# Layer 2's products of seven in a written order on all engines, with the fourth product later

## The chip, the cores and the metric

The kernel runs on one NeuronCore of a Trainium2 chip. TensorE (PE) multiplies matrices into PSUM banks, VectorE (DVE) and ScalarE (ACT) read those banks, GpSimd (POOL) works on SBUF only, and SyncE (SP) issues most DMAs. Each engine works through its own list of instructions in order and waits, where it must, for another engine. The metric is the device time of one execution in microseconds (us), as a median of runs.

## What is computed

Four layers work on x, 128 graphs of 64 nodes with 256 features; each is `x = layernorm(x + layer(x))`. Layer 0 is an attention over the adjacency, layer 1 an attention over 512 edges, layer 3 two graph convolutions and four LSTMs. The change lies in layer 2:

```python
agg = einsum('nm,bmd->bnd', A_hat, features)   # 8192 rows x 256
h   = relu(batchnorm(agg.reshape(-1, d) @ W1.T + b1, g1, be1))   # 256 -> 512
out = batchnorm(h @ W2.T + b2, g2, be2)                           # 512 -> 256
```

A batch norm takes mean and variance over all 8192 rows, so nothing behind it can start until every row has been multiplied and counted.

## The kernel before

**Blocks.** The 8192 rows stand transposed (features on partitions) as 16 blocks of 512 columns, `Aq(q)`, each with two halves of 128 features. The up multiplication makes `hidden(q, m)`, m = 0 to 3; the down multiplication makes `result(q, m)`, m = 0 and 1.

**Two ways to multiply.** A plain block (`up_block`, `up` and `put`, L721 to L742) takes 4 x 2 matmuls of 128 x 128 by 128 x 512; ACT adds the bias and DVE takes `bn_stats`. A job of seven (`class Seven`, L774, `seven`, L824) does a 2 x 2 by 2 x 2 product of tiles, for two blocks at once, with seven products instead of eight. It needs sums of the weight tiles (`weight_sums`, L747) and of the inputs (`tile_sums`, L833: three subtractions on POOL and one on DVE, in place). An up job (`up_job`, L846) has one term per product and covers one half g of the hidden features; a down job (`down_job`) has two terms, so two matmuls per product, and covers both results of two blocks.

**What the products need of each other.** Products 1 and 2 share one bank, products 6, 7 and 4 a second, products 5 and 3 a third. What ACT or DVE takes of a product has to be read before PE may add the next into that bank. Product 1 is copied by ACT (`kept`), product 6 is added to it by DVE (L801), product 5 is copied with its bias by ACT (L803), product 2 is finished by ACT (L805), product 3 by DVE (L808), product 7 by DVE (L812) and POOL (L813), product 4 by DVE (L816). The fourth product of a job is not done in that job: `seven` does it behind product 1 of the next job, from the list `late`. Each finished tile is counted by `bn_stats` on DVE (L849 up, L964 down).

**The order of the stages.** The program is written once, fully unrolled. Where nothing ties two instructions, a planner with its own estimates of durations fixes their order on each engine; `tc.issue_after` ties an instruction behind another on the same engine.

1. The last steps of layer 1 (`v_a`, `v_b`, `v_c`, the softmax of the last pair of blocks) are interleaved with entries of the list `fill`: plain blocks 0, 3, 4, 7, 8 and jobs for the pairs 1-2, 5-6 and 9-10. PSUM has five banks for them.
2. Plain block 11, then four up jobs: half 0 of pairs 12-13 and 14-15, then half 1 of both. From here there are eight banks. When the last job of a half has its fourth product, `finish` computes the scale and shift of batch norm 1 for that half (`normalisation`, L704).
3. `first(k)`, k = 0 to 3: the down multiplication of blocks 0 to 3, all eight banks open at once, one k after another. `relu` (L909, ACT) normalises and rectifies a tile in place. `prepare(4)` runs the relus and tile sums for the first down job beside it. At the end DVE takes the statistics and adds the bias (`leave`, L923).
4. Five down jobs for the pairs 4-5 to 12-13; during each one, `prepare` (or `ready`, for the last) is asked step by step for the relus and tile sums of the next pair. `done` stores both blocks to DRAM (`z_dram`, L968).
5. Plain down blocks 14 and 15, their statistics (L997), the bias additions (L923), `with_bias` (L930: the bias on the means) and `normalisation` of batch norm 2 for each half.
6. Layer 3 starts with the scale and shift of block 0 on ACT (L1144), transposes on PE (L1162), the addition to `x2r` (L1168), which SP loads from DRAM at that place (L1138), and a layer norm. All of layer 3 has its order written by hand by `given`, which ties every instruction behind the one called before it on its engine.

Of the kernel before, what the change touches and what calls it, by code (L numbers as in the profile page):

```python
# [41 lines left out]
def kernel(ctx: ExitStack, tc: tile.TileContext, i, out):  # L42
# [63 lines left out]
    bdT = const.tile([P, P], F32, name="bdT")  # L106

# [7 lines left out]
    with ExitStack() as two:  # L115
# [619 lines left out]
        def up_block(q):  # L735
            for m in range(2):
                put(q, m, up(q, m))
                if late:
                    late.pop(0).product(4)
            pz = [up(q, m) for m in (2, 3)]  # L740
            for m in (2, 3):
                put(q, m, pz[m - 2])  # L742
# [18 lines left out]
        kept_at = iter(range(10 ** 6))  # L761
# [12 lines left out]
        class Seven:  # L774

            def __init__(self, terms, bias, dst, stats, done=None, shape=lambda t: t):
                self.terms, self.bias, self.dst, self.stats, self.done = terms, bias, dst, stats, done
                self.shape = shape
                self.bank, self.kept = {}, {}

            def product(self, j):
                at = {1: 0, 2: 0, 6: 1, 7: 1, 4: 1, 5: 2, 3: 2}[j]
# [7 lines left out]
                self.use(j, self.bank[at])  # L790

            def keep(self, j):
                self.kept[j] = kept[next(kept_at) % len(kept)]
                return self.kept[j]

            def use(self, j, p_):
# [7 lines left out]
                elif j == 2:  # L804
                    nc.scalar.activation(dst(0, 0), shape(p_), AF.Identity, bias=self.bias(0))  # L805
                    self.stats(0, 0)
                elif j == 3:
                    nc.vector.scalar_tensor_tensor(dst(0, 1), shape(p_), self.bias(0), shape(k[6]),  # L808
                                                   op0=OP.add, op1=OP.add)
                    self.stats(0, 1)  # L810
                elif j == 7:
                    nc.vector.tensor_add(self.keep(7), p_, k[1])  # L812
                    nc.gpsimd.tensor_tensor(dst(1, 1), shape(k[7]), shape(k[5]), OP.add)  # L813
                    self.stats(1, 1)
                else:
                    nc.vector.scalar_tensor_tensor(dst(1, 0), shape(p_), self.bias(1), shape(k[1]),  # L816
                                                   op0=OP.add, op1=OP.add)
                    self.stats(1, 0)
                    if self.done:
                        self.done()  # L820
# [3 lines left out]
        def seven(job, feed=iter(())):  # L824
            job.product(1)
            if late:
                late.pop(0).product(4)
            for j in (6, 5, 2, 3, 7):
                job.product(j)
                next(feed, None)  # L830
            late.append(job)

# [9 lines left out]

        def inputs(q):
            return lambda k, n: Aq(q + n)[:, k * QT:(k + 1) * QT]

        def up_job(q, g, T, done=None):  # L846
# [4 lines left out]
                        lambda m: b1[:, 2 * g + m:2 * g + m + 1], dst, stats, done))  # L851
# [9 lines left out]
        fill = []  # L861
        for q in range(0, 8, 4):
            fill += [one(q), pair(q + 1, 0), one(q + 3), pair(q + 1, 1)]
        fill += [one(8), pair(9, 0), pair(9, 1)]
        sums_at = {0: 1, 4: 5, 8: 9}
        for n, (do, q) in enumerate([(v_b, NQ - LAG - 1), (v_c, NQ - LAG - 1)] + [
                (do, q) for q in range(NQ - LAG, NQ) for do in (v_a, v_b, v_c)]):
            if n in sums_at:
                T[sums_at[n]] = tile_sums(inputs(sums_at[n]))
            do(q, *[False] * (do == v_c))  # L870
            fill[n]()
# [8 lines left out]
        kept.append(wc.tile([P, QT], F32, name="kept4"))  # L880
# [12 lines left out]
        nc.sync.dma_start(bias2, i["L3_gnn_bhh"].rearrange("s (m p) -> p s m", p=P))  # L893

        assert q == NQ - LAST - 1
        up_block(q)
        ends = range(NQ - LAST, NQ, 2)
        T = {q: tile_sums(inputs(q)) for q in ends}
# [4 lines left out]
        for g in range(2):  # L903
            for q in ends:
                up_job(q, g, T[q], finish(g) if q == ends[-1] else None)
# [28 lines left out]
        def first(k):  # L934
            for q in range(LAST):
                relu(q, k)
                for m in range(M2):
                    if k == 0:
                        pz[q, m] = pbank()
                    down(q, m, pz[q, m], [k])  # L940
                    if late:
                        late.pop(0).product(4)
# [3 lines left out]
        def prepare(q):  # L946
            terms[q] = []
            for g in range(2):
                for k in range(2):
                    for n in range(2):  # L950
                        relu(q + n, 2 * g + k)
                    yield
                b = lambda k, n, g=g: hidden(q + n, 2 * g + k)
                a = lambda m, k, g=g: w2[:, 2 * g + k, m * P:(m + 1) * P]
                terms[q].append((a, [SW[1][:, n, g] for n in range(4)], b, tile_sums(b)))

        def ready(q):
            for k in range(M1):
                for n in range(2):
                    relu(q + n, k)  # L960
                yield

        def down_job(q, feed):
# [6 lines left out]
            seven(Seven(terms[q], lambda m: b2[:, m:m + 1], lambda m, n: result(q + n, m), stats, done, parts), feed)  # L970
# [4 lines left out]
        feed = prepare(LAST)  # L975
        for k in range(M1):
            first(k)
            next(feed, None)
        for _ in feed:
            pass  # L980
        for m in range(M2):
            for q in range(LAST):
                nc.vector.bn_stats(st2[:, m, q, :], pz[q, m])
                leave(q, m, pz[q, m])
            with_bias(m, 0, LAST)
        for q in range(LAST, NQ - 2, 2):
            down_job(q, prepare(q + 2) if q + 2 < NQ - 2 else ready(q + 2))
        ends = range(NQ - 2, NQ)
        pz = {}
        for m in range(M2):  # L990
            for q in ends:
                pz[q, m] = pbank()
                for k in range(M1):
                    down(q, m, pz[q, m], [k])
                    if late:
                        late.pop(0).product(4)
                nc.vector.bn_stats(st2[:, m, q, :], pz[q, m])  # L997
            if m == M2 - 1:
                for q in ends:
                    for n in range(M2):  # L1000
                        leave(q, n, pz[q, n])
            with_bias(m, NQ - 2, NQ)
            normalisation(sc2, sh2, st2, g2, be2, m)
# [18 lines left out]


    latest = {}

    def given(do, *args):
        traced = nc.cur_bb.bb.instructions
        first = len(traced)
        with ExitStack() as order:
            for e in latest.values():  # L1030
                order.enter_context(tc.issue_after(e))
            r = do(*args)
        for t in traced[first:]:
            if t.engine in (mybir.EngineType.PE, mybir.EngineType.DVE, mybir.EngineType.Activation,
# [615 lines left out]
```

## Time and profile before

| | us |
|---|---|
| three runs | 2067.59, 2071.39, 2072.15 |
| median | 2071.39 |
| profiled execution, its time | 2072.72 |
| profiled execution, its span | 2070.8 |
| mean granted clock | 0.982 |
| layer 2 in the trace, first to last matmul | 524.2 to 773.0 |

A row of the profile names a line of the kernel, an engine, an operation, and out<-in by the names of tiles. `pz` is a PSUM bank of layer 2, `Z` and `A` hold the hidden features, `SW` sums of weights, and `gath`, `lb`, `keep`, `wv`, `seg`, `w` and some of `Z` are rooms for the tile sums, taken over from layer 1. A float32 matmul stands as two records. A wait is put down to the instruction that ended it.

### The profile page before, as it was taken

Reading aid. Unit: us, or ns where it says so; the run is one execution under the profiler, and the core shown is the slowest. Engines: PE = TensorE matmul, PEld = TensorE weight load, DVE = VectorE, ACT = ScalarE, POOL = GpSimd, SP = SyncE. Lnnn points to the kernel's source line nnn. Section 1 sums busy time; section 2 is a strip of 40 time slices with the busy share of each in tenths; the row PEclk is TensorE's granted clock in tenths of the full one; section 3 lists DMA queues with packets and bytes.
Section 4 is the critical chain, followed back from the end, with each engine's and each line's share of the span. In section 5 each row is a group of like instructions: output and inputs, shape, how many; then the busy total and the mean of one; then the engine's idle time right before and its main releaser. Section 6 shows DMA issues by size and latency. Waiting matters only on the chain.

```text
span 2070.8 us, 31477 instructions
## 1 busy us (share of the span) xinstructions
PE 1961.5 (95%) x11579; PEld 1371.8 (66%) x11579; DVE 1209.8 (58%) x2702; ACT 959.9 (46%) x1840; POOL 808.4 (39%) x958
## 2 busy tenths in 40 slices
PE   5999999998899998999999999999999999999997
PEld 4666667675454335587678587687587687586675
DVE  7456666554567555574466674466674456443556
ACT  2766666665234713544343644343643343543333
POOL 1123343343534524273545253345253345123254
PEclk9999999999899998999999999999999999999998
DMA  5354343332202027351232532032522032301012
GB/s 148 66 69 70 72 76 53 55 54 44 34 21 39 24 93 245 130 191 52 87 132 68 183 113 92 11 131 69 182 86 79 1 119 71 128 1 76 1 62 72
DMA packets 235962, 170.69 MB, mean 82 GB/s; under 512 B 150560, under 2 KB 213536, under 8 KB 232480
## 3 DMA queue, kind: packets, MB, share of 16 engines
q1 hardware_dynamic: 233952, 166.72, 28.6%
q8 instruction: 91, 1.49, 0.3%
q0 software_dynamic: 1024, 1.05, 0.2%
q10 hardware_dynamic: 832, 0.92, 0.1%
q14 instruction: 63, 0.52, 0.1%
HBM read 107.82 MB, written 60.82 MB: 81 GB/s over the span
## 4 chain that ended last, share of the span: by engine, by line
PE 71%; DVE 14%; ACT 5%; POOL 4%; issue 3%; DMA 2%; SPq 1%; DVEq 0%; ACTq 0%; POOLq 0%
PE l L1392 26%; PE l L1357 9%; PE l L1249 8%; PE pz L788 4%; PE e L331 3%; PE m L303 2%; PE g L1212 2%; PE m L306 2%; PE z L340 2%; PE pz L727 2%; PE m L238 2%; PE m L421 2%; PE g L1127 1%; DVE cell L1336 1%; PE g L1200 1%
## 5 line engine op out<-in xcount | busy, mean ns | idle before, releaser
L1392 PE MATMUL l<-xs,wx 128*128 128x256 f32 (+1 forms) x896 | 276.8, 399 | 5.1 <-DVE gate L1411 3.9
L1392 PE MATMUL l<-hs,wh 128*128 128x256 f32 (+1 forms) x896 | 275.1, 399 | 3.1 <-DVE hs L1286 3.1
L86 POOL TENSOR_TENSOR ln_rs<-ln_rs,mhalf 128x2 f32<-128x2 f32 (+2 forms) x98 | 84.0, 857 | 436.8 <-DVE ln_rs L98 423.9
L1407 ACT ACTIVATE kept<-l 128x256 f32<-128x256 f32 (+1 forms) x224 | 88.6, 402 | 339.9 <-PE l L1392 338.6
L1392 PE MATMUL l<-H,wx 128*128 128x256 f32 (+1 forms) x672 | 210.2, 401 | 3.4 <-DVE gate L1420 3.4
L1392 PE MATMUL l<-hid,wh 128*128 128x256 f32 (+1 forms) x672 | 208.7, 399 | 0.0
L1392 PEld LDWEIGHTS l<-xs,wx 128*128 128x128 f32 x896 | 168.8, 190 | 49.5 <-POOL st L100 4.1
L1392 PEld LDWEIGHTS l<-hs,wh 128*128 128x128 f32 x896 | 169.3, 190 | 45.5 <-DVE hs L1286 5.7
L1357 PE MATMUL l<-H,wx 128*128 128x256 f32 (+1 forms) x768 | 187.9, 403 | 6.2 <-DVE H L1322 6.2
L1425 ACT ACTIVATE gate<-gate,bias 128x512 f32<-128x512 f32 (+1 forms) x280 | 170.5, 656 | 37.0 <-DVE gate L1416 31.0
L1357 PEld LDWEIGHTS l<-H,wx 128*128 128x128 f32 x768 | 146.8, 193 | 46.4 <-DVE H L1322 10.4
L1249 PE MATMUL l<-H,wih 128*128 128x512 f32 x384 | 167.9, 598 | 2.6 <-issue 2.6
L342 ACT ACTIVATE u<-z 128x1024 f32<-128x1024 f32 x128 | 130.4, 1025 | 63.2 <-PE z L340 62.1
L1392 PEld LDWEIGHTS l<-H,wx 128*128 128x128 f32 x672 | 126.0, 190 | 38.4 <-DVE gate L1420 7.3
L1392 PEld LDWEIGHTS l<-hid,wh 128*128 128x128 f32 x672 | 127.2, 190 | 32.0 <-issue 2.9
L1249 PEld LDWEIGHTS l<-H,wih 128*128 128x128 f32 x384 | 73.3, 192 | 93.2 <-issue 86.7
L1415 POOL TENSOR_TENSOR gate<-gate,kept 128x256 f32<-128x256 f32 (+1 forms) x84 | 65.2, 776 | 158.6 <-DVE kept L1413 158.6
L314 DVE TENSOR_TENSOR qs<-m,qs 64x256 fp32r<-64x256 f32 x128 | 54.0, 422 | 109.2 <-ACT qs L313 107.1
L1290 POOL TENSOR_TENSOR hs<-hid 128x256 f32<-128x256 f32 (+1 forms) x28 | 25.7, 916 | 200.0 <-DVE hid L1319 116.3
L340 PE MATMUL z<-gath_r,qs 128*128 128x512 f32 x256 | 100.5, 479 | 0.4 <-ACT u L342 0.2
L1344 ACT ACTIVATE gate<-cell 128x512 f32<-128x512 f32 (+1 forms) x88 | 58.6, 666 | 81.1 <-DVE cell L1336 58.8
L1409 DVE TENSOR_TENSOR gate<-l,kept 128x256 f32<-128x256 f32 (+1 forms) x112 | 49.1, 438 | 72.2 <-ACT gate L1425 44.1
(346 smaller groups left out, 3837.2 us busy)
## 6 DMA issues: line engine op xcount, KB each, us to landing
wx<-sums SPq DMA_DIRECT2D x9, 2048.0 KB
wh<-sums SPq DMA_DIRECT2D x9, 1792.0 KB
way<-st SPq DMA_DIRECT2D x54, 256.0 KB
st<-way SPq DMA_DIRECT2D x216, 64.0 KB
xin<-in_x SPq DMA_DIRECT2D x16, 512.0 KB
ld<-table SPq DMA_DIRECT2D x16, 512.0 KB
x_dram<-y SPq DMA_DIRECT2D x16, 512.0 KB
x2r<-x_dram SPq DMA_DIRECT2D x32, 256.0 KB
```

The lines of the kernel that those rows point to most:

```text
L86: nc.gpsimd.tensor_tensor(dst, dst, mhalf[:, :n], OP.pow)
L331: nc.tensor.matmul(pes[S][n * CG:(n + 1) * CG, :], apad[:, k, CG - HEADS - r0:2 * CG - HEADS - r0], u[:, k, :], start=r0 == 0 and k == 0, ...
L340: nc.tensor.matmul(z[:, k, :], L1[q]["qs"][c][:, s, k * P:(k + 1) * P], gath_r, start=True, stop=True)
L342: nc.scalar.activation(u, z, AF.Relu)
L788: nc.tensor.matmul(self.bank[at], lhs, rhs, start=first and n == 0, stop=n == len(self.terms) - 1, skip_group_check=True)
L1249: nc.tensor.matmul(b, wih1[:, k, mw * P:(mw + 1) * P], Hw[:, k], start=k == 0, stop=k == KD - 1)
L1344: nc.scalar.activation(tiles["g"][m], cell[:, m], AF.Tanh)
L1357: nc.tensor.matmul(one, w.raw[0][:, k, at, m, :], inp(r, 0, k)[:, g], start=k == 0, stop=k == KD - 1)
L1392: nc.tensor.matmul(self.banks[j], lhs, rhs, start=src == 0, stop=src == 1)
L1407: nc.scalar.activation(self.keep(j), b, AF.Copy)
L1415: e.tensor_tensor(t[0][:, 1], t[0][:, 1], k[5], OP.add)
L1425: given(lambda: nc.scalar.activation(dst, dst, f, bias=b))
```

## The change

- `given` moves to the top of the kernel, and with it layer 2 from block 11 on gets a written order on PE, DVE, ACT and POOL: each product, what is read of it, each relu, each sum and each statistic.
- Beside layer 1 there are seven plain blocks, 0 to 6, and the pairs 7-8 and 9-10.
- The fourth product and its two last statistics come later: in an up job behind product 5, in a down job behind product 6. `seven` takes them in steps (`tail`) from the job before.
- In an up job the third product is left to ACT and POOL instead of DVE. `kept` tiles have fixed places.
- The sums of the inputs of a down job come in two steps (`sums_in_order`), each in its place among the products. The relus of a pair are asked for in pairs, in six steps per job.
- In `first`, statistics and `leave` come block by block in the last k. In the last two blocks, block 14 leaves early, and block 15 is left by ACT behind the last normalisation in the program.
- `x2r` of blocks 0 and 1 is loaded while layer 2 runs.

```diff
+    latest = {}
+
+    def given(do, *args, **more):
+        traced = nc.cur_bb.bb.instructions
+        first = len(traced)
+        with ExitStack() as order:
+            for e in latest.values():
+                order.enter_context(tc.issue_after(e))
+            r = do(*args, **more)
+        for t in traced[first:]:
...
+                latest[t.engine] = t
+        return r
...
+            def tail(self):
+                self.product(4)
+                yield self.counted(1, 1)
+                yield self.counted(1, 0)
+                if self.done:
+                    self.order(self.done)
...
         def seven(job, feed=iter(())):
+            rest = late.pop(0).tail() if late else iter(())
             job.product(1)
-            if late:
-                late.pop(0).product(4)
-            for j in (6, 5, 2, 3, 7):
-                job.product(j)
-                next(feed, None)
+            next(feed, None)
+            job.product(6)
+            if len(job.terms) > 1:
+                next(rest, None)
+            next(feed, None)
+            job.product(5)
+            next(rest, None)
+            next(feed, None)
+            job.product(2)
+            for _ in rest:
+                pass
+            next(feed, None)
+            job.product(3)
+            job.counted(0, 0)
+            next(feed, None)
+            job.product(7)
+            job.counted(0, 1)
+            next(feed, None)
             late.append(job)
...
+        def sums_in_order(b):
+
+            t2, t3, t4 = rooms[next(rooms_at) % len(rooms)]
+            t1 = b(0, 1)
+            given(nc.gpsimd.tensor_tensor, t3, b(1, 1), t1, OP.subtract)
+            yield
+            given(nc.vector.tensor_sub, t1, t1, b(0, 0))
+            given(nc.gpsimd.tensor_tensor, t2, b(1, 1), t1, OP.subtract)
+            given(nc.gpsimd.tensor_tensor, t4, b(1, 0), t2, OP.subtract)
+            yield [t1, t2, t3, t4]
...
-        for q in range(0, 8, 4):
-            fill += [one(q), pair(q + 1, 0), one(q + 3), pair(q + 1, 1)]
-        fill += [one(8), pair(9, 0), pair(9, 1)]
-        sums_at = {0: 1, 4: 5, 8: 9}
+        fill = [one(n) for n in range(7)] + [pair(n, g) for n in (7, 9) for g in range(2)]
+        sums_at = {4: 7, 6: 9}
...
+        early = {n: load_x2(n) for n in range(2)}
...
-                up_job(q, g, T[q], finish(g) if q == ends[-1] else None)
+                up_job(q, g, T[q], finish(g) if q == ends[-1] else None, order=given)
...
+                    given(down, q, m, pz[q, m], [k])
+                    if k == M1 - 1:
+                        given(nc.vector.bn_stats, st2[:, m, q, :], pz[q, m])
+                        if m:
+                            for n in range(M2):
+                                given(leave, q, n, pz[q, n])
...
             for g in range(2):
                 for k in range(2):
                     for n in range(2):
-                        relu(q + n, 2 * g + k)
-                    yield
+                        given(relu, q + n, 2 * g + k)
+                    if k == 0:
+                        yield
...
-                terms[q].append((a, [SW[1][:, n, g] for n in range(4)], b, tile_sums(b)))
+                T = sums_in_order(b)
+                yield next(T)
+                terms[q].append((a, [SW[1][:, n, g] for n in range(4)], b, next(T)))
+                if g == 0:
+                    yield
...
-                nc.vector.bn_stats(st2[:, m, q, :], pz[q, m])
-            if m == M2 - 1:
-                for q in ends:
+                given(nc.vector.bn_stats, st2[:, m, q, :], pz[q, m])
+                if m and q == ends[0]:
                     for n in range(M2):
-                        leave(q, n, pz[q, n])
-            with_bias(m, NQ - 2, NQ)
-            normalisation(sc2, sh2, st2, g2, be2, m)
+                        given(leave, q, n, pz[q, n])
+            given(with_bias, m, NQ - 2, NQ)
+            given(normalisation, sc2, sh2, st2, g2, be2, m)
+        for m in range(M2):
+            given(nc.scalar.activation, result(q, m), parts(pz[q, m]), AF.Identity, bias=b2[:, m:m + 1])
+        nc.sync.dma_start(z_dram[q], Aq(q))
...
-        x2r = []
-        for a in range(2):
-            x2r.append(work.tile([P, 2, D], F32, name="x2r", bufs=4))
-            nc.sync.dma_start(x2r[a].rearrange("p c d -> p (c d)"), x2_dram[q][:, a * 2 * D:(a + 1) * 2 * D])
+        x2r = early.pop(q, None) or load_x2(q)
```

## The prediction

> **What bounds the kernel now.** I read the page first, then the work of each engine in seven stretches around layer 2, TensorE's waits there, the timeline of one joint, and the granted clock after idle times.
>
> ```profile
> span 2070.8 us, 31477 instructions
> PE 1961.5 (95%) x11579; PEld 1371.8 (66%) x11579; DVE 1209.8 (58%) x2702; ACT 959.9 (46%) x1840; POOL 808.4 (39%) x958
> ```
>
> TensorE (PE) is busy for 95% of the span, so only its idle times, its number of matmuls and its clock can move the end. The stretches (columns: stretch, its length, then busy us of PE, PEld, DVE, ACT, POOL, granted clock, DMA) are: layer 1's tail with blocks beside it (two lines), the last up jobs, the first down blocks, the five down jobs, the last two blocks, and the entry of layer 3.
>
> ```profile
> 523.20:551.50 28.30, 20.36 (x118) 10.95 (x114) 17.62 (x30) 5.57 (x10) 19.21 (x18) 0.88 0.06 23
> 551.50:636.70 85.20, 85.19 (x586) 43.73 (x587) 58.23 (x105) 29.25 (x46) 36.30 (x37) 1.00 0.27 50
> 636.70:664.00 27.30, 25.64 (x58) 10.01 (x57) 20.60 (x40) 14.33 (x22) 4.95 (x5) 1.00 0.00 0
> 664.00:695.40 31.40, 30.21 (x71) 13.00 (x69) 15.55 (x28) 28.97 (x42) 18.22 (x15) 1.00 0.00 1
> 695.40:757.20 61.80, 57.81 (x133) 24.90 (x134) 39.37 (x53) 20.24 (x31) 28.66 (x22) 1.00 0.17 68
> 757.20:773.00 15.80, 15.78 (x37) 6.53 (x35) 7.68 (x15) 1.09 (x2) 1.81 (x2) 1.00 0.20 81
> 773.00:790.00 17.00, 8.93 (x83) 6.40 (x83) 10.52 (x34) 3.66 (x7) 4.47 (x8) 0.60 0.68 226
> ```
>
> Length less PE's time is what can be won: 7.9, 0, 1.7, 1.2, 4.0, 0 and 8.1 us. ACT is full in the fourth stretch and one third full in the fifth: all rectifications (relu, L909) are done ahead. PE's waits from 640 to 775 us (total, times, longest):
>
> ```profile
> PE pz L788 <- DVE kept L812: 4.7, 4, 1.3
> PE pz L788 <- DVE A L923: 1.2, 1, 1.2
> PE pz L788 <- ACT kept L803: 0.5, 2, 0.3
> ```
>
> The first line is a fourth product that follows too soon on VectorE's read of the seventh (0.9 us in the up jobs, 1.28, 1.20 and 1.29 at the joints of the down jobs). One joint, as a timeline:
>
> ```profile
> 671.59 8.57 ACT L909 ACTIVATE A<-A,sh,sc 128x512 f32<-128x512 f32 x12 [2.43 <-DVE sh L712]
> ...
> 730.98 1.27 POOL L837 TENSOR_TENSOR seg<-Z 128x512 f32<-128x512 f32 x1 [3.75 <-PE pz L788]
> 732.21 1.26 POOL L837 TENSOR_TENSOR Z<-A 128x512 f32<-128x512 f32 x1
> 732.28 1.73 DVE L838 TENSOR_TENSOR Z<-Z,Z 128x512 f32<-128x512 f32 x1 [0.72 <-POOL seg L837]
> 734.10 1.27 POOL L839 TENSOR_TENSOR wv<-Z 128x512 f32<-128x512 f32 x1 [0.63 <-DVE Z L838]
> ...
> 740.85 1.02 PE L788 MATMUL pz<-A,w 128*128 128x512 f32 x2
> 741.97 0.69 ACT L805 ACTIVATE A<-pz,b 128x512 f32<-128x512 f32 x1 [1.04 <-PE pz L788]
> ```
>
> A relu costs 8.57/12 = 0.714 us. L838 (alone 0.69) takes 1.73 while POOL works: it ends 0.54 after POOL's subtraction (733.47). One matmul, two records here, advances PE by 0.86; ACT starts 0.25 after that slot (741.97 against 740.85 + 0.86).
>
> **The change, part by part.** The sum is made against the profiled execution (2072.72 us: span 2070.8 and 1.9 around it), 1.3 above the median 2071.39; differences are then set on the median.
>
> *Fill beside layer 1.* Before: five blocks of 8 matmuls and six jobs of 7, 82; after: seven and four, 84. Two matmuls: +1.72. The wait of 0.73 for ACT's kept (550.78) belonged to a job that is no longer there: -0.73. The 4.88 us at 527.8 wait for layer 1's softmax on DVE; in it a tile sum's L838 waited 1.77 for POOL and ran 0.69 ahead of a scan. The tile sums of block 7 are free to rise to the same place, so I take 0; bounds -2.5 (both gone) and +1.3 (one more POOL addition of 1.27 ahead of a layer norm). Sum +1.0. That the third product's addition leaves DVE for ACT (0.69) and POOL (1.27) is hidden: DVE has 4.85 us of work per up job of 6.0, ACT 2.7, POOL 2.5.
>
> *Last up jobs, in a given order.* The fourth product follows the fifth, 2.58 us behind the seventh; DVE's read needs about 1.1. The waits of 0.42, 0.90 and 0.34 go: -1.66. What is late next: `finish` of half 0 sits in DVE's list ahead of the third job's statistics and its read of product 7. Its chain, from the rows at 653.27 to 658.19 without what lay between, is two aggregations 0.55, two POOL powers 0.56 and six small steps: 3.4 us. It starts 5.7 us into the job, the read ends at 10.5, PE wants product 4 at 8.6: +2.0 (0.7 if the two chains interleave). And no relu can start before ACT has left the last job's product 3: 0.25 + 0.69 + 0.71 + 0.1 behind it, less product 7's 0.86: +0.9. Sum +1.2.
>
> *First down blocks.* `leave` is done per block, so the banks are free in time: -1.22. DVE has 16 steps of 0.69 = 11.1 us in the last 6.9 us of PE and ends some 7 us behind PE, but job 4's sixth product must be read only 8.6 us behind: hidden. `finish` of half 1 has 10 us of PE work as cover; the relus of blocks 4 and 5 (8 x 0.71) fit into ACT's 27 us.
>
> *Down jobs.* The fourth product comes one product later: -3.77. A job's two stores of z (512 KB each, SP) go out behind the next job's product 2; their first reader is the load at 797, so nothing waits. But the second half's relus of the next job are now placed behind product 2's leaving, and ACT runs in order. From the end of product 2: ACT 0.25 + 0.69, four relus 2.86 = 3.8; POOL's first subtraction to 5.1; POOL's own addition for product 7, next in its list, to 6.4; L838 cannot pass it, 6.9; POOL's second subtraction to 8.2, PE sees it at 8.3. PE wants that sum in the second matmul of product 6: products 3 and 7, 3.44, product 1, 1.72, one matmul 0.86 = 6.0. PE waits 2.3 us, and since the chain hangs on product 2 of the same job it does so in each of jobs 6, 8, 10 and 12: +9.2. (Job 4's sums come from the blocks before, at about 1.9 against 2.6 us: just in time.) Bounds of one wait: 0 (all relus ahead, as before) and 2.7 (L838 and an addition both at the held 1.7). Sum +5.4.
>
> *Clock.* Idle times of this length cost more than themselves here (two stretches, then one joint of the down jobs):
>
> ```profile
> 809.93:813.34 3.41, 0.78 (x4) 0.37 (x3) 3.31 (x10) 0.44 (x1) 3.10 (x6) 1.00 0.25 81
> 813.34:816.75 3.41, 3.41 (x5) 1.35 (x4) 3.11 (x13) 0.51 (x1) 2.40 (x5) 0.50 0.70 222
> 706.40:709.80 3.40, 2.12 (x6) 1.06 (x6) 2.59 (x3) 1.95 (x4) 2.77 (x3) 1.00 0.00 0
> 709.80:713.20 3.40, 3.40 (x9) 1.52 (x8) 2.63 (x4) 0.00 (x0) 3.40 (x4) 1.00 0.62 249
> ```
>
> After 2.63 us idle the clock is 0.50 for 3.41 us, a loss of 1.7; after 1.28 it is not. The same stands after idle times of 2.07, 2.25, 2.53 and 2.75 us elsewhere. The half clock comes and goes on a grid of 3.41 us, so a wait split by the grid may go free. Five waits of 2.0 to 2.3: I take half of them, 2.5 x 1.7 = +4.3; bounds 0 and 8.5. The Trainium skill ("TensorE: Matmul & The Clock Gate", section "Why this matters for your kernels") asks only for no idle gaps over about 3 us; by that rule this term is 0 and the forecast 2076.3, but the row at 2.63 us already contradicts it, and the row decides.
>
> *End of layer 2.* Block 15's bias additions (L923 twice, 1.39 us) leave DVE's list ahead of the last normalisation, ACT does them beside it: from PE's end 773.02 the scale starts at 3.0 instead of 4.2. The loads of x2r for 0 and 1 (landed 779.9) go ahead, four DMAs on SP behind weight loads and nothing urgent behind them. They landed just as the transposes ended, so they give nothing alone: -1.2, up to -2.3 if the matmul with `ones` also gets off the path. I take -1.5.
>
> Sum: 1.0 + 1.2 - 1.2 + 5.4 + 4.3 - 1.5 = +9.2: 2081.9 for the profiled execution, 2080.6 on the median.
>
> **Rivals.** *Faster:* the second half's sums come in time, because ACT or POOL have less in front of them than I read. Then the sum is 1.0 + 1.2 - 1.2 - 3.8 - 1.5 = -4.3 and 2067.1. It decides where one wait in the down jobs is under 4.3/4 = 1.07 us. For it: ACT has 4 us of slack per job; against it: the chain of 8.3 us is made of rows, and ACT's slack lies ahead of product 2.
> *Waits without the clock:* the five waits fall across the grid; +4.9, 2076.3; with the softmax wait shortened by 2.5 as well, 2073.8, within 0.2%. For it: 1.28 us idle kept the clock.
> *Every wait halves the clock, some for two periods* (6.8 us, as after the 2.07 and 2.25 us idle times): 2071.4 + 4.9 + 8.5 = 2084.8 to about 2090.
>
> **How the numbers follow.** About 0.2% (4.1 us) is what a measurement here can tell. Forecast with its partial clock loss 0.40, every wait at half clock 0.20, waits without the clock 0.16 (half of it within 0.2%), faster 0.19, something else of either sign 0.05. Faster 0.21, same 0.13, slower 0.66. The slower cases alone span 2076 to 2090; with the faster rival the range is 2066 to 2090.
>
> **What would show it.** Right: PE waits of about 2.3 us on POOL's L839 successor, four times, at the second matmul of product 6; relus in pairs between ACT's evictions instead of one full stretch; half-clock spells between 690 and 765 us; waits on L812 at the joints and on L923 gone; ACT's first scale of the last half about 3 us behind PE's end. Wrong: no wait on POOL in the down jobs, or the early 4.88 us shrunk.

## The result and the profile after

| | before | after |
|---|---|---|
| median of 8 runs, us | 2070.53 (2067.59 to 2073.82) | 2078.30 (2076.28 to 2080.65) |
| profiled execution, its time | 2072.72 | 2077.86 |
| profiled execution, its span | 2070.8 | 2076.1 |

The ratio is 1.0037 [1.0026, 1.0048]: the changed kernel is slower, by 7.8 us on the medians. The profile explains 5.3 us of them, the difference of the two spans; the profiled execution of before lies 2.2 us above its median and that of after 0.4 below, so the rest is the scatter of single executions. Below, one execution of old_fill (2135.84 us) and one of joined (2913.3 us) that ran in a slower state are left out.

The page of the kernel after, its first line and the busy times:

```profile
span 2076.1 us, 31444 instructions
PE 1964.1 (95%) x11583; PEld 1374.2 (66%) x11583; DVE 1193.1 (57%) x2683; ACT 968.7 (47%) x1852; POOL 809.6 (39%) x961
```

DVE has lost 16.7 us of work, ACT has gained 8.8 and PE four records (two matmuls). None of this shows where the time went. Four stretches do (columns as in the prediction): from layer 1's last scores to the first of the last up jobs, the up jobs, layer 2's down part to PE's last matmul, and the entry of layer 3 up to its first graph matmul.

```profile
522.57:638.65 116.08, 107.57 (x710) 56.09 (x707) 65.67 (x120) 39.81 (x62) 54.04 (x54) 0.99 0.23 43
638.65:665.35 26.70, 24.14 (x56) 9.83 (x54) 20.56 (x39) 12.11 (x20) 9.26 (x9) 1.00 0.09 34
665.35:781.18 115.83, 107.06 (x238) 45.90 (x238) 56.94 (x94) 54.05 (x78) 47.61 (x40) 0.97 0.12 48
781.18:789.22 8.04, 2.28 (x10) 1.65 (x11) 6.19 (x22) 5.41 (x10) 1.87 (x4) 0.73 0.59 209
```

The same stretches of the kernel before, cut at the same instructions:

```profile
523.24:637.59 114.35, 106.40 (x706) 55.05 (x703) 76.32 (x135) 35.48 (x56) 55.51 (x55) 0.97 0.22 43
637.59:663.97 26.38, 24.72 (x56) 9.60 (x55) 20.11 (x39) 13.65 (x22) 4.95 (x5) 1.00 0.00 0
663.97:773.02 109.05, 103.86 (x239) 44.45 (x237) 62.63 (x95) 50.34 (x74) 48.69 (x39) 1.00 0.13 51
773.02:783.37 10.35, 2.62 (x12) 1.97 (x11) 7.41 (x24) 3.06 (x6) 1.87 (x4) 0.63 0.79 270
```

The lengths differ by +1.73, +0.32, +6.78 and -2.31 us; what lies ahead of them and behind gives -1.2, together the +5.3 of the spans. The third stretch alone is longer by more than the whole difference. TensorE's waits of the kernel after from 640 to 785 us (total, times, longest):

```profile
PE pz L813 <- POOL wv L116: 4.4, 2, 2.2
PE pz L813 <- POOL Z L116: 4.4, 2, 2.2
PE g L1181 <- DVE st L1179: 3.3, 1, 3.3
PE pz L813 <- DVE wq L838: 1.9, 1, 1.9
PE pz L983 <- ACT Z L979: 0.6, 1, 0.6
```

The waits on `kept` and on `leave` that the prediction showed are gone. In their place PE waits four times, 2.2 us each, for a sum that POOL makes; L116 is the inner call of `given`, under which the instructions passed to it directly stand. The timeline of the first of these joints:

```profile
700.98 0.69 ACT L829 ACTIVATE A<-pz,b 128x512 f32<-128x512 f32 x1 [1.08 <-PE pz L813]
701.57 2.92 ACT L979 ACTIVATE A<-A,sh,sc 128x512 f32<-128x512 f32 x4
...
704.56 1.27 POOL L116 TENSOR_TENSOR Z<-A 128x512 f32<-128x512 f32 x1 [0.68 <-ACT A L979]
...
705.79 1.26 POOL L839 TENSOR_TENSOR A<-wq,kept 128x512 f32<-128x512 f32 x1
...
705.86 1.74 DVE L116 TENSOR_TENSOR A<-A 128x512 f32<-128x512 f32 x1 [0.30 <-POOL Z L116]
...
707.68 1.27 POOL L116 TENSOR_TENSOR Z<-A 128x512 f32<-128x512 f32 x1 [0.63 <-DVE A L116]
...
709.00 1.38 PE L813 MATMUL pz<-Z,SW 128*128 128x512 f32 x2 [2.19 <-POOL Z L116]
```

It is one chain: product 2 leaves on ACT, behind it four relus, behind them POOL's first subtraction, POOL's own addition for product 7, a subtraction on DVE that runs 1.74 us beside it, POOL's second subtraction, and then PE. Each step starts when the one above it ends, but for the subtraction on DVE: it starts beside POOL's own addition, behind the first subtraction, and ends 0.55 us behind that addition.

The clock of the four joints, in windows of one period of 3.41 us that hold (most of) the wait, and the period after each:

```profile
706.33:709.74 3.41, 1.22 (x4) 0.49 (x3) 1.27 (x1) 3.07 (x5) 2.70 (x3) 1.00 0.38 154
709.74:713.15 3.41, 3.41 (x5) 1.35 (x4) 0.69 (x1) 0.00 (x0) 1.78 (x2) 0.50 0.00 0
723.39:726.80 3.41, 1.62 (x4) 0.87 (x5) 0.78 (x2) 2.18 (x4) 2.87 (x3) 1.00 0.38 154
726.80:730.21 3.41, 3.41 (x9) 1.52 (x8) 2.45 (x5) 0.35 (x1) 0.90 (x1) 1.00 0.16 66
737.05:740.46 3.41, 1.22 (x3) 0.49 (x3) 1.20 (x1) 3.00 (x5) 2.70 (x3) 1.00 0.38 154
740.46:743.88 3.42, 3.42 (x5) 1.35 (x4) 0.69 (x1) 0.00 (x0) 1.70 (x2) 0.50 0.00 0
754.11:757.53 3.42, 1.71 (x4) 0.87 (x5) 0.79 (x2) 2.11 (x3) 2.54 (x2) 1.00 0.38 153
757.53:760.94 3.41, 3.41 (x9) 1.52 (x8) 2.16 (x4) 0.44 (x1) 0.00 (x0) 1.00 0.18 74
```

The four waits are equally long. Where a wait lay whole in one period (PE busy 1.22 of 3.41, so 2.19 idle) the next ran at half clock; where the grid cut it (1.79 and 1.71 idle in the period) the clock stayed. Two half periods cost 2 x 1.7 = 3.4 us in this execution; where the grid falls differs between executions (in that of old_fill below only one wait of the four lies whole in a period).

### The profile page after: what moved, and what is told of

Same layout as the page of the kernel before. It is cut to its first block, busy times and chain, and to the rows that moved or that the text cites. A ratio compares the mean times of both kernels' runs of the same rounds, so it can differ in the third digit from the quotient of the medians.

```text
span 2076.1 us, 31444 instructions
## 1 busy us (share of the span) xinstructions
PE 1964.1 (95%) x11583; PEld 1374.2 (66%) x11583; DVE 1193.1 (57%) x2683; ACT 968.7 (47%) x1852; POOL 809.6 (39%) x961
## 3 DMA queue, kind: packets, MB, share of 16 engines
q0 software_dynamic: 1024, 1.05, 0.2%
## 4 chain that ended last, share of the span: by engine, by line
PE 58%; DVE 9%; POOL 4%; issue 2%; ACT 1%; DMA 1%; SPq 0%; POOLq 0%; DVEq 0%; ACTq 0%
PE l L1474 27%; PE l L1439 9%; PE l L1331 8%; PE pz L813 4%; PE pz L742 2%; PE g L1294 2%; PE pz L983 2%; PE g L1212 1%; PE g L1282 1%; DVE cell L1418 1%; DVE gate L1417 1%; DVE ln_st L95 1%; DVE kept L1495 1%; ACT A L979 1%; POOL gate L1497 0%
## 5 line engine op out<-in xcount | busy, mean ns | idle before, releaser
L1439 PEld LDWEIGHTS l<-H,wx 128*128 128x128 f32 x768 | 146.8, 193 | 46.4 <-DVE H L1404 10.4
```

Of the source, the lines that this page charges most:

```text
L1439: nc.tensor.matmul(one, w.raw[0][:, k, at, m, :], inp(r, 0, k)[:, g], start=k == 0, stop=k == KD - 1)
```

## Experiments

The theory: the relus of the next pair, placed behind product 2's leaving, and POOL's own addition make a sum late four times, and half of these waits cost clock on top. The main rival: the loss comes from elsewhere (the new order beside layer 1, the last up jobs, the fourth product's place), and the waits only take up slack. The times of before in each row are those of the same chip; the runs took four chips, and equal values of before mean the same one. The ratios are the recorded ones; they differ by up to 0.0010 (joined) from the quotient of the two medians.

| run | median us | before us | ratio |
|---|---|---|---|
| relu_ahead | 2065.23 | 2072.08 | 0.9968 [0.9956, 0.9979] |
| sum_first | 2068.05 | 2072.08 | 0.9980 [0.9971, 0.9989] |
| one_more | 2088.17 | 2072.08 | 1.0081 [1.0066, 1.0095] |
| old_fill | 2074.89 | 2072.08 | 1.0012 [1.0003, 1.0020] |
| joined | 2060.69 | 2067.59 | 0.9957 [0.9945, 0.9970] |
| ahead_finish | 2059.25 | 2067.59 | 0.9952 [0.9939, 0.9964] |
| ahead_no_early | 2064.51 | 2067.59 | 0.9981 [0.9972, 0.9989] |
| ahead_bias_first | 2065.27 | 2067.59 | 0.9982 [0.9972, 0.9992] |
| ahead_old_x2 | 2067.76 | 2070.74 | 0.9987 [0.9978, 0.9996] |
| ahead_third_dve | 2060.57 | 2070.74 | 0.9951 [0.9937, 0.9964] |
| together | 2061.89 | 2070.70 | 0.9961 [0.9947, 0.9974] |
| together_old_fill | 2061.03 | 2070.70 | 0.9960 [0.9946, 0.9974] |

### relu_ahead: the relus of the second half ahead of product 2

```diff
                     for n in range(2):
                         given(relu, q + n, 2 * g + k)
-                    if k == 0:
-                        yield
+                if g == 0:
+                    yield
...
                 T = sums_in_order(b)
+                if g:
+                    yield
                 yield next(T)
                 terms[q].append((a, [SW[1][:, n, g] for n in range(4)], b, next(T)))
-                if g == 0:
-                    yield
```

> The changed kernel, but the second half's four relus of the next pair are asked for behind product 5 instead of behind products 2 and 3, so that ACT does them before it takes product 2. Theory (ACT's list sets the waits of 2.19 us): the sum is ready about 0.6 us before PE wants it, the four waits on POOL go (8.8 us) and with them the two half-clock spells of 3.41 us in the down jobs (3.4 us): 12.2 us less than the changed kernel's 2078.3, about 2066, ratio to before about 0.998. Rival (POOL is the limit of the down jobs, whatever ACT does): waits of about 1 us stay and 2071 or more. Rival (the time lies elsewhere, in the fill or in layer 3): the waits go and the time stays within 3 us of 2078.

Measured 0.9968 [0.9956, 0.9979]: the change goes from slower than before to faster. The edit does more than the expectation names. With the four relus, both steps of the second half's sums move up by one product (as does one pair of the first half's relus), so in POOL's list the awaited subtraction now stands ahead of POOL's own addition for product 7. Both things that lay in the chain are out at once. The timeline of the same joint:

```profile
699.61 2.92 ACT L979 ACTIVATE A<-A,sh,sc 128x512 f32<-128x512 f32 x4
...
702.43 0.67 ACT L829 ACTIVATE A<-pz,b 128x512 f32<-128x512 f32 x1
...
703.66 1.27 POOL L116 TENSOR_TENSOR Z<-A 128x512 f32<-128x512 f32 x1
...
705.79 1.27 POOL L116 TENSOR_TENSOR Z<-A 128x512 f32<-128x512 f32 x1 [0.87 <-PE pz L813]
...
707.12 1.13 PE L813 MATMUL pz<-Z,SW 128*128 128x512 f32 x2 [0.49 <-POOL Z L116]
...
708.37 1.28 POOL L839 TENSOR_TENSOR A<-wq,kept 128x512 f32<-128x512 f32 x1
```

The relus run first, product 2 leaves behind them, and POOL's own addition no longer lies between the two subtractions. PE waits 0.49 us here and at none of the other three joints. The windows of this kernel's down part and of the entry of layer 3:

```profile
665.16:768.52 103.36, 102.87 (x238) 44.97 (x238) 52.77 (x94) 53.59 (x78) 47.73 (x40) 1.00 0.13 53
768.52:776.88 8.36, 2.58 (x11) 1.96 (x11) 6.19 (x22) 5.40 (x10) 1.86 (x4) 0.68 0.58 218
```

The down part takes 103.36 us in place of 115.83, and PE is busy for 102.87 of them: 12.5 us gone, of which the waits were 8.77 - 0.49 = 8.3 and the half clock 3.4; 0.8 is left. A wait is counted from the end of a record of 1.02 us, and a matmul advances PE by 0.86, so each costs 0.16 more than is counted: with three waits fewer, 0.5 of the 0.8. It is also 5.7 us shorter than before's 109.05, which is what the rest of the change brings in this part. The rival that the loss comes from elsewhere falls.

### sum_first: only POOL's own addition behind the sums

```diff
                     nc.vector.tensor_add(self.keep(7), p_, k[1])
-                    nc.gpsimd.tensor_tensor(dst(1, 1), shape(k[7]), shape(k[5]), OP.add)
+                    if len(self.terms) == 1:
+                        self.joined()
...
             job.counted(0, 1)
             next(feed, None)
+            if len(job.terms) > 1:
+                job.order(job.joined)
```

> The changed kernel, but POOL's own addition for product 7 stands behind the next pair's sums in POOL's list instead of between them; the relus stay where they are. Theory: the chain loses that one addition, 1.24 us, and L838's counterpart on DVE runs in 0.69 instead of 1.74 us, so the waits shrink from 2.19 to about 1.0 us, too short for the half clock: 4 x 1.2 + 3.4 = 8.2 us less, about 2070, ratio 1.000. If the clock does not hang on the length of the waits: half-clock spells stay and about 2073.5. Rival (the waits come from ACT alone): 2.19 us each and 2078 stay.

TensorE's waits of this kernel from 640 to 785 us, the two lines on POOL's sums:

```profile
PE pz L813 <- POOL Z L116: 2.3, 2, 1.2
PE pz L813 <- POOL wv L116: 2.1, 2, 1.1
```

The relus stay late, one addition of 1.27 us leaves the chain, and each wait falls from 2.19 to between 1.05 and 1.21. At that length no half period follows. From the wait in the up jobs to the end of layer 2 it takes 114.57 us where the change takes 122.36, 7.8 less: 4.4 of waits and 3.4 of clock. The late relus alone, without POOL's addition in the chain, cost far less. No run moves the relus alone; what they cost by themselves is known only as these waits of 1.05 to 1.21 against 0.49 once in relu_ahead.

The run came out 2 us below its expectation of 2070 and beats before, but not in layer 2: from the start of the wait for layer 1's softmax to PE's last matmul of layer 2 it takes 246.2 us, before 245.2, the change 254.1 and relu_ahead 241.5. It wins behind that. Its entry of layer 3 takes 7.7 us, that of before 10.4. And later in layer 3, which the edit does not touch, the trace of the change has a period at half clock from 1887.34 and one from 1969.26, that of before from 1881.71 and 1963.63, and this one has none there. Two such periods cost up to 3.4 us. So part of what this execution wins over that of before is clock and not order.

### one_more: one subtraction more in the same place

A superfluous subtraction on POOL ahead of the awaited one, into a tile that a later subtraction overwrites; it is asked for in the second half's sums only.

```diff
-        def sums_in_order(b):
+        def sums_in_order(b, more=0):
...
             given(nc.vector.tensor_sub, t1, t1, b(0, 0))
+            if more:
+                given(nc.gpsimd.tensor_tensor, t4, b(1, 1), t1, OP.subtract)
             given(nc.gpsimd.tensor_tensor, t2, b(1, 1), t1, OP.subtract)
...
-                T = sums_in_order(b)
+                T = sums_in_order(b, g)
```

> The changed kernel with one POOL subtraction more (1.24 us, its result written over later) ahead of the awaited sum in jobs 4 to 10. Theory: each of the four waits grows from 2.19 to about 3.4 us, +5.0, and now every one of them fills enough of a clock period to be followed by half clock, two spells more or longer ones, +3.4: about 2086.5, ratio about 1.008. If the clock does not follow the waits: +5.0 alone, 2083. Rival (the waits are not on the path that sets the end): 2078.

TensorE's waits of this kernel from 640 to 785 us, and one joint's two periods in windows:

```profile
PE pz L813 <- POOL wv L116: 6.8, 2, 3.4
PE pz L813 <- POOL Z L116: 6.8, 2, 3.4
```

```profile
758.98:762.39 3.41, 0.56 (x2) 0.00 (x0) 1.36 (x1) 3.15 (x5) 2.78 (x3) 1.00 0.38 154
762.39:765.80 3.41, 2.83 (x4) 1.29 (x5) 0.65 (x1) 0.00 (x0) 1.79 (x2) 0.50 0.00 0
```

Each wait grows from 2.19 to 3.41, by an addition's length: this chain sets the end there, and no other path ends close behind it. This joint has the most favourable cut of the four, 2.85 us idle in the period, and still the clock halves. All four waits cost clock now: 4 x 1.22 + 2 x 1.7 = 8.3 us; the spans differ by 8.6.

### old_fill: the former order of blocks beside layer 1

```diff
-        fill = [one(n) for n in range(7)] + [pair(n, g) for n in (7, 9) for g in range(2)]
-        sums_at = {4: 7, 6: 9}
+        fill = []
+        for q in range(0, 8, 4):
+            fill += [one(q), pair(q + 1, 0), one(q + 3), pair(q + 1, 1)]
+        fill += [one(8), pair(9, 0), pair(9, 1)]
+        sums_at = {0: 1, 4: 5, 8: 9}
...
+            if n in sums_at:
+                T[sums_at[n]] = tile_sums(inputs(sums_at[n]))
             do(q, *[False] * (do == v_c))
             fill[n]()
-            if n in sums_at:
-                T[sums_at[n]] = tile_sums(inputs(sums_at[n]))
```

> The changed kernel with the list beside layer 1 as before it: blocks 0, 3, 4, 7, 8 and the pairs 1, 5, 9. Theory: two matmuls less, -1.72, and one wait for ACT's copy back, +0.73, the softmax wait of 4.88 us as it is: 1.0 us less, about 2077.3, ratio 1.0032. Rival (the blocks also shield PE from layer 1's waits): equal or up to 2 us slower. Rival (the sums and additions of the old list delay layer 1's softmax): the 4.88 us change by over 1 us.

From the start of the softmax wait to the start of the wait in the up jobs it takes 130.04 us where the change takes 131.69: -1.65. (Behind the softmax wait PE runs at half clock, in every run, for one or two periods as the grid falls; by PE's busy time in them that costs 2.0 us here, 1.7 in the change. Differences of 0.4 us between stretches that begin there say nothing.) Two matmuls (1.72) and a wait of 0.75 at 622 us went, and the wait of 0.74 for ACT's `kept` that before has is back: 1.72 + 0.75 - 0.74 = 1.73. The wait of 4.89 for the softmax is the same in both. The four waits in the down jobs are 2.19 here as well, but only one of them (738.30) is followed by half clock, since the grid falls otherwise; so this run's whole time holds 1.7 us that belong to the clock and not to the fill. One trace does not settle why its ratio, 1.0012, came out below the 1.0032 expected.

### ahead_third_dve: the up jobs' third product back on DVE

On top of relu_ahead:

```diff
-                    if len(self.terms) == 1:
+                    if False:
                         nc.scalar.activation(dst(0, 1), shape(p_), AF.Identity, bias=self.bias(0))
                         nc.gpsimd.tensor_tensor(dst(0, 1), dst(0, 1), shape(k[6]), OP.add)
```

> The kernel of relu_ahead with the up jobs' third product left to DVE in one instruction, as before the change, instead of ACT and POOL. Theory: DVE has 5.6 us of work in an up job of 6.0, so no wait arises in the plain jobs; behind the scale and shift of half 0 PE's wait of 1.85 grows by 0.75 to 2.6 and may be followed by half clock (1.7); the wait of 0.62 for the first relu goes. Sum +0.1, or +1.8 with half clock: 2065.3 to 2067, ratio 0.9969 to 0.9977. Rival (DVE becomes the bound of the up jobs): waits in every job, 2070 or more.

From the softmax wait to the end of layer 2 it takes 239.70 us where relu_ahead takes 241.53: DVE gets work back and the kernel is 1.8 us shorter, which the expectation had the other way round. The reason stands in DVE's list. In the kernel after, ahead of a layer norm that PE waits for (0.75 us at 622), and at the scale of batch norm 1:

```profile
613.84 0.69 DVE L912 BATCH_NORM_STATS2 st<-A 128x6 f32<-128x512 f32 x1 [0.51 <-POOL A L833]
615.07 1.74 DVE L890 TENSOR_TENSOR A<-A 128x512 f32<-128x512 f32 x1 [0.53 <-POOL lb L889]
616.73 0.68 DVE L438 TENSOR_TENSOR y<-m,A 128x512 f32<-128x512 f32 x1
...
622.81 2.08 PE L456 MATMUL m<-aht,y 64*64 64x64 f32 x64 [0.75 <-POOL y L100]
...
657.75 1.28 POOL L833 TENSOR_TENSOR A<-A,kept 128x512 f32<-128x512 f32 x1
657.82 1.21 DVE L725 TENSOR_TENSOR sc<-sc,g 128x1 f32<-128x1 f32 x1 [0.37 <-POOL sc L86]
```

The same places in ahead_third_dve:

```profile
613.48 0.68 DVE L912 BATCH_NORM_STATS2 st<-A 128x6 f32<-128x512 f32 x1
614.08 1.63 DVE L890 TENSOR_TENSOR A<-A 128x512 f32<-128x512 f32 x1
615.63 0.68 DVE L438 TENSOR_TENSOR y<-m,A 128x512 f32<-128x512 f32 x1
...
656.69 0.16 DVE L725 TENSOR_TENSOR sc<-sc,g 128x1 f32<-128x1 f32 x1 [0.37 <-POOL sc L86]
```

With POOL's addition (L833) in the way, the statistic behind it waits on an engine that works in order, and all of DVE's list stands behind it; POOL's next work, a subtraction that DVE waits for too, is late by the same addition: the layer norm starts 1.1 us later. At the scale, a product of 128 numbers takes 1.21 us beside POOL's addition and 0.16 without it. The wait of 0.75 at 622 is gone, that of 1.85 in the up jobs is 1.45, and in place of the 0.62 for a relu there is one of 0.32 for the last job's read: 1.45 of the 1.83 us. The medians differ by 4.7, more than the stretch: of the 4.2 between the two spans 2.6 lie behind layer 2, where relu_ahead's trace has a half-clock period from 1874.00 and one from 1955.92 and this one none.

### ahead_finish: batch norm 1's scale behind the read of product 7

On top of relu_ahead, in the up jobs:

```diff
                 if self.done:
+                    yield
                     self.order(self.done)
...
             job.product(2)
-            for _ in rest:
-                pass
+            next(rest, None)
+            if len(job.terms) > 1:
+                for _ in rest:
+                    pass
...
             job.counted(0, 1)
+            for _ in rest:
+                pass
```

> The kernel of relu_ahead with batch norm 1's scale and shift for half 0 moved behind the third up job's read of product 7. Theory: PE's wait of 1.85 us in the last up jobs goes, its wait of 0.62 us on the first relu stays: 2063.4, ratio 0.996. Rival (the wait only moves): 2065.2, ratio 0.9968.

The wait of 1.85 us on the read of product 7 goes. Where the 0.62 for a relu was, there are now 0.17 for a read, 0.19 for the relu and 0.59 for the last job's read; 240.07 us to the end of layer 2, 1.46 less than relu_ahead. The profiled execution, 2064.03 us, is the highest of five, so its trace does not show what the median of 2059.25 has beyond that.

### joined, together, together_old_fill

`joined` has relu_ahead, old_fill and ahead_finish's edit; `together` has relu_ahead, ahead_finish's edit and the third product on DVE; `together_old_fill` adds the former fill to that. Their edits are those shown above:

```diff
+        fill += [one(8), pair(9, 0), pair(9, 1)]
...
+                    yield
                     self.order(self.done)
...
+                    if False:
```

> The kernel of relu_ahead (2065.2, ratio 0.9968) with the old list beside layer 1 and with batch norm 1's scale and shift for half 0 moved behind the third up job's read of product 7. Theory: 1.7 us less for two matmuls, 1.85 us less for the wait of PE on DVE before that job's product 4: about 2061.7, ratio about 0.995. Rival (the 1.85 us only move to the first relu, which needs that scale): 2063.5, ratio 0.996.

> The changed kernel with three edits: the second half's relus ahead (relu_ahead), the scale and shift of half 0 behind the read of product 7 (ahead_finish), the up jobs' third product on DVE (ahead_third_dve). Theory: the waits they remove are different ones, 0.0032 + 0.0016 + 0.0017 of the time below 1, but the last two share the wait of 1.85 us and what is left of it: ratio 0.994, about 2058.3 against a before of 2070.7. Rival (the last two are one gain): 0.995.

> The kernel of together with the old list beside layer 1 (two matmuls fewer). Theory: 1.7 us less, ratio 0.0008 below that of together. Rival (the old list brings a wait of 0.73 for ACT's copy and the same waits on layer 1): 1.0 less or equal.

The gains do not add up. `joined` saves 1.59 us more than ahead_finish between the softmax wait and the end of layer 2 (238.48), 0.4 of it half clock in layer 1, but its time cannot be told from that of ahead_finish. `together` takes 239.50 us there, hardly less than either of its parts. The first wait of the up jobs is gone, and PE waits 1.71 us for the fourth product of the last job. The read that it waits for, of `together` first and of ahead_third_dve second:

```profile
663.62 0.67 DVE L838 TENSOR_TENSOR wq<-pz,kept 128x512 f32<-128x512 f32 x1
```

```profile
663.64 0.68 DVE L838 TENSOR_TENSOR wq<-pz,kept 128x512 f32<-128x512 f32 x1
```

It starts at the same time with `finish` in either place (the two stretches start within 0.2 us of each other): from 653 us on DVE has no idle time until then but two waits of 0.51 and 0.37 for POOL inside `finish`, in both. The order of its work moves the wait from one job to the fourth product of the next; only less work on DVE would shorten it.

### ahead_bias_first, ahead_old_x2, ahead_no_early: the entry of layer 3

All on top of relu_ahead: the bias additions of block 15 back on DVE ahead of the normalisation; `x2r` in layer 3's own pool and loaded there, as before; and the early calls alone taken out.

```diff
-                if m and q == ends[0]:
+                if m:
                     for n in range(M2):
                         given(leave, q, n, pz[q, n])
...
-        for m in range(M2):
-            given(nc.scalar.activation, result(q, m), parts(pz[q, m]), AF.Identity, bias=b2[:, m:m + 1])
-        nc.sync.dma_start(z_dram[q], Aq(q))
```

```diff
-        wx = ctx.enter_context(tc.tile_pool(name="wx", bufs=4, side="right", reuse_waits="tile"))
...
-        early = {n: load_x2(n) for n in range(2)}
...
-        x2r = early.pop(q, None) or load_x2(q)
+        x2r = []
+        for a in range(2):
+            x2r.append(work.tile([P, 2, D], F32, name="x2r", bufs=4))
+            nc.sync.dma_start(x2r[a].rearrange("p c d -> p (c d)"), x2_dram[q][:, a * 2 * D:(a + 1) * 2 * D])
```

```diff
-        early = {n: load_x2(n) for n in range(2)}
+        early = {}
```

> The kernel of relu_ahead with block 15's bias additions on DVE ahead of the last statistics' normalisation, as before the change; the early loads stay. Theory: two additions of 0.7 us lie in the chain again, the first scale on ACT starts 4.3 instead of 3.0 us behind PE's last matmul: 1.3 us more, 2066.5, ratio 0.9975. Rival (something else, such as the matmul with ones, holds the start of layer 3): 2065.2.

> The kernel of relu_ahead with x2r in layer 3's own pool and loaded where layer 3 asks for it, as before the change. (In ahead_no_early the planner still sent the loads at 634.9 us, since their pool was free; that run took nothing away.) Theory: the loads queue on SP behind the store of block 15 and land about 6.2 us behind PE's last matmul, where the transposes are done at 4.6: the next wait of PE ends 1.6 us later, 2066.8, ratio about 0.9976. Rival (a tie, as the prediction read it in the trace of before): no change, 0.9968.

> The kernel of relu_ahead without the early loads of x2r for blocks 0 and 1; they are issued on SP where layer 3 asks for them, behind the store of block 15. Theory: the store waits for ACT until 1.5 us behind PE's last matmul, the load lands 4.4 us after its issue at about 1.8, so the first addition to x2r starts at 6.2 instead of 4.6 us behind PE's end: 1.6 us more, 2066.8, ratio 0.9976. Rival (as before the change, the load is no later than the transposes): 2065.2.

From PE's last matmul of layer 2 to the first graph matmul relu_ahead takes 8.36 us, ahead_bias_first 9.55 (+1.19) and ahead_old_x2 9.22 (+0.86). ahead_no_early tells nothing: the tiles' pool was free, the planner raised the loads to 634.9 us without being asked (634.5 in relu_ahead), and the stretch is 8.36 again. It does show how far ratios carry: what is in effect one kernel has 0.9968 on one chip and 0.9981 on another. By time, neither ahead_bias_first (0.9982) nor ahead_old_x2 (0.9987) can be told from these two; the two differences are read from the traces, one execution each. What the early loads give is seen at the addition to `x2r`, in ahead_old_x2:

```profile
774.33 0.69 DVE L1242 TENSOR_TENSOR x2r<-g,x2r 128x512 f32<-128x512 f32 x1 [1.11 <-DMA x2r<-x_dram]
```

and in relu_ahead, where it waits only for the transposes on PE:

```profile
773.49 0.69 DVE L1250 TENSOR_TENSOR x2r<-g,x2r 128x512 f32<-128x512 f32 x1 [0.24 <-PE g L1244]
```

## Why the prediction was right, and where it was not

*Down jobs.* Right, in place, mechanism and size. The chain after the end of product 2 was put at 3.8, 5.1, 6.4, 6.9, 8.2 and 8.3 us; in the joint shown, with product 2's slot ending at 700.64, it ran 3.85, 5.2, 6.4, 7.0, 8.3 and 8.4. Four waits of 2.19 against 2.3. relu_ahead and sum_first together show that the two things named, the relus behind product 2 and POOL's own addition, are what makes them; the addition was taken out alone, the relus only together with it. one_more shows that no other path lies close behind the chain.

*Clock.* Right in kind: 3.4 us against 4.3. The waits in the down jobs cost half of what they could, as taken, but that is the luck of this execution: the grid decides which, in old_fill's it was one of four. The fifth wait, 1.85 us in the up jobs, cost none. The Trainium skill ("TensorE: Matmul & The Clock Gate", section "Why this matters for your kernels") asks for no idle gaps over about 3 us; gaps of 2.19 us halved the clock here. By the time alone the rival "waits without the clock" (2076.3) lies as near to the median of 2078.3 as the forecast (2080.6); the two half periods behind two of the waits are what tells them apart. "Every wait halves the clock" fell with the other two.

*First down blocks.* Right: the waits on `leave` are gone and nothing took their place. With the down jobs and their clock, -1.2 + 5.4 + 3.4 (the clock term for four of the five waits) = +7.6 was foreseen for the third stretch, +6.8 was measured.

*Last up jobs.* The mechanism was right, the size too large: waits of 1.85 for the read behind `finish` (2.0 foreseen) and 0.62 for a relu (0.9) came for the 1.66 that went, +0.8; the stretch grew by 0.3. The other 0.5 lies in PE's busy time of 56 records each, whose ends are modelled, and stays open.

*Fill.* Here a step failed: "That the third product's addition leaves DVE for ACT (0.69) and POOL (1.27) is hidden". It was counted as load, and DVE's load falls; but the statistic of that tile now waits for POOL, and DVE's list waits with it. That is the 0.75 us at 622 (ahead_third_dve), and +1.73 in place of +1.0. It takes the new order of blocks as well: old_fill, with the same addition on POOL, has no wait there. The softmax wait stayed at 4.88, as taken.

*End of layer 2.* Right in direction, too small: "They landed just as the transposes ended, so they give nothing alone" failed. It compared the landing, 779.9 in the kernel before, with the end of all eight transposes (780.03); but the first addition needs only the first four. In relu_ahead it starts 1.10 us behind the first transpose, which in the kernel before would have been 779.10, where it started at 779.97. The row said so, with 1.11 us of waiting for the DMA:

```profile
779.97 0.69 DVE L1168 TENSOR_TENSOR x2r<-g,x2r 128x512 f32<-128x512 f32 x1 [1.11 <-DMA x2r<-x_dram]
```

So the early loads are worth 0.86 and the bias additions 1.19. Measured -2.3 against -1.5. That is the bound given, but not for its reason: the matmul with `ones` (L1181) still stands directly ahead of the transposes. About 0.3 of the 2.3 is clock, since relu_ahead, with the half clock as early as in before, needs 8.36 where the change needs 8.04. The first scale starts 3.05 us behind PE's end, as foreseen.

The *faster* rival is what relu_ahead is: with every sum but one in time the change runs at 0.9968 of before, which on the median of the prediction is 2064.8; the rival had 2067.1. Its break point was 1.07 us per wait; sum_first's waits of 1.05 to 1.21 came out at 0.998 instead. The terms around them (fill, up jobs, entry of layer 3) make 1.0 us less than foreseen, and the two half-clock periods in layer 3 that sum_first's trace lacks up to 3.4; one trace of each does not settle how much of this the medians hold.

## What to carry to other kernels

When an order is written by hand, follow the longest chain through all engines from the last instruction that it must stand behind to the first that wants its result, and compare it with the work that PE has in between: here 8.3 us against 6.0. An instruction taken off a busy engine is not off its path if the next in that engine's list reads its result. Put long work that is ready early (relus) ahead of the short eviction that a chain begins with, and work that nobody waits for (POOL's own addition) behind the sums that PE wants. The best versions, ahead_third_dve and ahead_finish, take 0.995 of before; in their traces they are 1.8 and 1.5 us shorter than relu_ahead from the softmax wait to the end of layer 2, and what their medians lead by beyond that the traces do not show.

## What the runs showed of the hardware

- In the down jobs a period of the 3.41 us grid with 2.19 us or more of PE idle was followed by half clock every time (2.19 in the change and in old_fill, 2.85 to 3.20 in one_more), one with 1.79 us or less never. Waits of the same length thus cost 2.2 or 3.9 us, by where they fall. In layer 1, where the matmuls are smaller, a period with 1.55 us idle was followed by half clock in relu_ahead (512.09 to 515.50) and one with 1.55 was not in sum_first (514.62 to 518.03), so PE's idle time in a period does not decide alone.
- A product of 128 x 1 numbers on DVE took 1.21 us beside an addition on POOL and 0.16 without; a subtraction of 128 x 512 took 1.74 against 0.69. The small one ended with POOL's instruction (659.03), the large one 0.55 us behind it. Not all of DVE's work is held: in the change a statistic took 0.68 beside a subtraction on POOL (704.88), and a product's read from PSUM 0.75 (702.56).
